# Later normalisations in layer 0, and the sums at the boundary of two layers split anew between VectorE and GpSimd

## The chip, the cores and the metric

The kernel runs on one core of a Trainium2 chip. A core has five engines, each with its own in-order program: TensorE (PE in the profile, its weight loads PEld), VectorE (DVE), ScalarE (ACT), GpSimd (POOL), and SyncE (SP), which here issues nearly all DMAs. Engines wait for each other by semaphores. The metric is the device time of one execution in microseconds.

## The reference

The input `x` is 128 graphs of 64 nodes with 768 features, in float32, and `adj` a 64x64 mask for each graph. Two layers follow each other; both end in a residual and a layer normalisation.

```python
# layer 0, per graph (12 heads of 64)
h    = einsum('bnd,ade->bane', x, W);  th = tanh(h)
attn = th @ w_src + swapaxes(th @ w_dst)          # one score per pair of nodes
attn = where(~adj, -999, leaky(attn, 0.2));  attn = softmax(attn)
out  = elu(attn @ h + b)
gate = sigmoid(x @ H_w.T + H_b)
x    = layernorm(x + gate * out + (1 - gate) * x)
# layer 1, per graph (6 heads of 128)
q, k, v = x @ Wq + bq, x @ Wk + bk, x @ Wv + bv
probs   = softmax(q @ k.T / sqrt(128) + where(adj, 0, -9e15))
x       = layernorm(x + (probs @ v) @ Wf + bf)
```

## The kernel before

**Order.** All work is issued by hand-written step tables: `at(step, f)` puts a function into the list of a step, and `run` (L263) calls the lists in order. Within a step the order of the `at` calls counts. Since every engine is in order, this list is each engine's program; a function put a step later stands behind all that the earlier step issues on the same engine. A step of layer 0 holds one block product of TensorE (six matmul records of 128x384, about 1.94 us); a step of layer 1 has two pairs of 128x256 matmuls.

**Layer 0 (`phase_a`, L308).** The 8192 rows are 64 tiles of 128 rows (two graphs each), taken as 32 pairs. Each pair has three big products: h (with W), the gate, and, once the pair's layer 0 output is there, V (v of layer 1, with Wv). Each is done as a Winograd-form product in 7 block products (`Product`, L197): `matmuls(i)` and `evict(i)`, where ScalarE keeps one operand as `snap` (L418), and VectorE adds (L441 for h and gate, L460 for V). Pairs 0 to 2 start 14 steps apart (there is no V yet), later ones 21.

A tile then runs through the class `Tile0` (L469): tanh (L478), products with w_dst and w_src on GpSimd (L482, L490), the destination scores go through DRAM and come back spread over the rows (L500, L508, `dst_in`), neighbours' values of h come by DMA (`hx`, L518 and L519), twelve additions on ScalarE (L532, in two halves of six), mask and maximum (L539, L543, VectorE), exp (L548, ScalarE), scale by the reciprocal `rs` (L556, L558, GpSimd), probs (transposes on TensorE, L569, copied by L574), aggregate (L587, TensorE), elu (L601 to L615), two mixes with the gate (L620 to L630), the statistics of the norm (`norm1`: L284 to L295 on VectorE, L296 to L301 on GpSimd, which ends in `shift`), the normalisation itself (`norm2`: L305 on ScalarE, L639 on VectorE for the last pair), and the spill of the result to DRAM (`spill`, L647, x_d<-xb). About a pair later `x1_in` reads the rows back (L390, four DMAs of xp<-x_d a tile), they are transposed (L397; L412 and L413 for the last pair), stored as xT_d (L736) and feed the V product, whose results are stored by L461 (v_d<-v). `load(p)` (L337) reads x of a later pair.

**The boundary.** Layer 1's q, k and final products use another bilinear form: a weight has 15 slots of which 14 are sums (`weight15_sum`, L165 to L167; 128x512 elements each, columns of two halves, j = 0 and 1), and the activations have 11 sums (`group_sum`, L844 to L846, for a group of four tiles; `pair_sum`, L858, for pairs ahead of the final product). Before, the 14 sums of Wq run on VectorE and those of Wk on GpSimd, from step o+44 of the last pair (o is its first step), during its V product; the sums of Wf run on GpSimd in layer 1, from step 16. Chunks of the weights come by DMA (`load15`, L156).

**Layer 1 (`phase_b`, L789).** 16 groups, each with 90 steps: q and k of head halves j = 0, then j = 1 (`R` = 15 steps each), then the final products of its predecessor's context. A step's matmuls (L876) read a sum or part; results are taken by ScalarE (`first`, L897) or added by VectorE (`add`, L902). Scores are L941. `load_adj` also makes `fill` (L811) from the mask. For group 0 the sums were spread over its first steps, four steps ahead of the step that needs them; group 1 has six of its sums on VectorE and five on GpSimd, all later groups all on GpSimd. The result buffers `X` in PSUM are shared by both layers and are given out in turn.

Since the change adds lines, some lines stand further down in the changed kernel: L736 becomes L741, L811 L819, L846 L854, L876 L884, L897 L905, L902 L910, L1113 L1125.

Of the kernel before, what the change touches and what calls it, by code (L numbers as in the profile page):

```python
# [12 lines left out]
ALU = mybir.AluOpType  # L13
AX = mybir.AxisListType

P = 128
# [3 lines left out]
L1_NEG = -9000000000000000.0  # L20
# [33 lines left out]
SIGN = {"+": ALU.add, "-": ALU.subtract}  # L54
# [7 lines left out]
def kernel(  # L62
# [84 lines left out]
    def weight15(i):  # L147
        return wts.tile([P, 7, CH, HALF], F32, name=f"w{i}", tag=f"w{i}").rearrange(
            "p s c o -> p (s c o)"
        )[:, : 15 * 2 * 256].rearrange("p (s c o) -> p s c o", s=15, c=2)  # L150

    def load15(wb, src, k):

        kb, c = divmod(k, 2)
        rows = src[k * P : (k + 1) * P, :] if src is Wf else in_order(src)[k]
        nc.sync.dma_start(  # L156
            wb[:, 3 * kb : 3 * kb + 3, c, :], rows.rearrange("p (n o) -> p n o", n=3)
        )
# [3 lines left out]
        r = src.rearrange("(h p c) o -> h c p o", h=2, c=CH)  # L162
        return [r[k // CH, k % CH] for k in range(NC)]

    def weight15_sum(wb, k, eng):  # L165
        to, a, b, sign = WEIGHT_SUMS[k]
        eng.tensor_tensor(wb[:, to], wb[:, a], wb[:, b], SIGN[sign])  # L167

    def weight_sums(part, eng, ks=range(4)):

# [137 lines left out]
    def phase_a(ctx):  # L308
# [24 lines left out]
        def load(p):  # L333
            st[p]["x"] = []
            for i in range(2):
                t = xb[:, (0, 1, 5, 6)[(2 * p + i) % 4]]
                nc.sync.dma_start(t, x_t[2 * p + i])  # L337
                st[p]["x"].append(t)
# [312 lines left out]
        def at(step, *fs):  # L651
            events.setdefault(max(step, 0), []).extend(fs)

        def dense(d, key, i):
            d[key].matmuls(i)
            d[key].evict(i)
# [19 lines left out]
        for p in range(NP):  # L676
            d, o = st[p], O[p]
            d["p"] = p
            if p:
                at(max(o - 20, 1), lambda p=p: load_adj(p))  # L680
                at(o + 8, lambda p=p: load(p))

            def xb_in(d, i):
                d.setdefault("xp", []).append(blocks(x_t[2 * d["p"] + i]))

            def xT(d, i):
                d.setdefault("T", []).append(turn(d["xp"][i]))

            if p:
                at(max(o - 20, 1), lambda d=d: xb_in(d, 0))  # L690
                at(max(o - 16, 1), lambda d=d: xb_in(d, 1))
                at(o - 6, lambda d=d: xT(d, 0))
                at(o - 5, lambda d=d: xT(d, 1))
                at(o - 4, lambda d=d: sums(d))
            else:
                at(0, lambda d=d: d.update(T=[transposed(t) for t in d["x"]]))
                at(0, lambda d=d: sums(d))
            at(o, lambda d=d: start_h(d))
            at(o + 7, lambda d=d: start_g(d))
            for i in range(7):  # L700
                at(o + i, lambda d=d, i=i: dense(d, "W", i))
                at(o + 7 + i, lambda d=d, i=i: dense(d, "G", i))
            for i, s in ((1, o), (0, o + (4 if p == NP - 1 else 5))):
                t = Tile0(p, i)
                at(s + 6 + (i == 0), t.tanh, t.cap)
                at(s + 7, t.dst_mul)
                at(s + 8, t.src_mul)
                at(s + 9, t.dst_sum, t.dst_out)
                at(s + 10, t.src_sum)
                at(s + 13, t.dst_in)  # L710
                at(s + 16, t.exchange)

                at(s + (15 if i else 17), lambda t=t: t.add(0))
                at(s + (16 if i else 17), lambda t=t: t.add(1))
                at(o + (14 if i else 16), t.gate_in)
                at(o + (17 if i else 18), t.gate)
                n = s - (i == 1)
                at(n + 18, t.mask, t.top)
                at(n + 19, lambda t=t: t.exp(0))
                at(n + 20, lambda t=t: t.exp(1))  # L720
                at(s + 21, lambda t=t: t.scale(0), lambda t=t: t.scale(1))
                at(s + 24, t.probs)
                at(s + 25, t.aggregate)
                at(s + 26, t.elu)
                at(s + 27, t.mix1)
                at(s + 28, t.mix2)
                at(s + 29, t.norm1)
                at(s + 30, t.norm2)
                at(s + 31, t.spill)

            def x1_in(d, i):
                d["xp", i] = blocks(x1_d[2 * d["p"] + i])

            def x1T(d, i, t):
                d["x1T", i] = t
                nc.sync.dma_start(xT_d[d["p"]][:, i], t)  # L736

            def x1_sums(d):
                d["T"] = [d["x1T", i] for i in range(2)]
                sums(d)  # L740

            if p < NP - 3:
                v = O[p + 3] + 14
                times = ((1, v - 19, v - 13), (0, v - 16, v - 10))
            elif p < NP - 1:

                v = O[-1] + (21 if p == NP - 3 else 28)
                times = ((1, v - 16, v - 7), (0, v - 15, v - 6)) if p == NP - 3 else (
                    (1, v - 12, v - 7), (0, v - 10, v - 6)
                )  # L750
            if p < NP - 1:
                for i, t0, t1 in times:
                    at(t0, lambda d=d, i=i: x1_in(d, i))
                    at(t1, lambda d=d, i=i: x1T(d, i, turn(d["xp", i])))
                at(times[1][2] + 1, lambda d=d: x1_sums(d))
            else:
                v = o + 45
                for i in range(2):
                    at(o + 43 - i, lambda d=d, i=i: x1T(d, i, transposed(d["x"][i])))
                at(o + 44, lambda d=d: x1_sums(d))  # L760
            at(v, lambda d=d: start_v(d))
            for i in range(7):
                at(v + i, lambda d=d, i=i: dense(d, "V", i))
# [6 lines left out]
        early = []  # L770

        def load_early(i, src, k):
            if k == 0:
                early.append(weight15(i))
            load15(early[i], src, k)

        for k in range(NC):
            at(o + (7 + k if k < 4 else 8 + 2 * k), lambda k=k: load_early(0, Wq, k))
            at(o + 20 + 2 * k, lambda k=k: load_early(1, Wk, k))
        for k in range(len(WEIGHT_SUMS)):  # L780

            at(o + 44 + k // 2, lambda k=k: weight15_sum(early[0], k, nc.vector))
            at(o + 45 + k // 2, lambda k=k: weight15_sum(early[1], k, nc.gpsimd))
        at(o + 30, lambda: load_T4(0))
        run(events, O[-1] + 80)
        return early
# [2 lines left out]
    def phase_b(ctx, wq, wk):  # L789
# [15 lines left out]
        def load_adj(g):  # L805
            d = st[g]
            a = small.tile([P, 2, 2, S], U8, name="adj1")
            for q in range(2):
                nc.sync.dma_start(a[:, q], adj_p[2 * g + q])
            d["fill"] = small.tile([P, 2, 2, S], F32, name="fill1")  # L810
            nc.vector.tensor_scalar(  # L811
                d["fill"], a, 1.0, -L1_NEG, op0=ALU.subtract, op1=ALU.mult
            )

        def load_v(g, q, i):
# [252 lines left out]
        def at(step, *fs):  # L1068
            events.setdefault(max(step, 0), []).extend(fs)
# [4 lines left out]

        R = len(STEPS)
        N = 6 * R
        wf = weight15(2)
        for k in range(NC):
            at(2 + k, lambda k=k: load15(wf, Wf, k))
        for k in range(len(WEIGHT_SUMS)):  # L1080
            at(16 + 2 * k, lambda k=k: weight15_sum(wf, k, nc.gpsimd))
        for g in range(NG):
            d, o = st[g], N * g
            d["S"] = {}
# [1 line left out]
            if g:  # L1086
                at(o - 29 if g > 1 else 14, lambda g=g: load_T4(g))
                at(o - 35, lambda g=g: load_adj(g))
            ready = {}
            for k in range(len(SUMS)):  # L1090


                eng = nc.vector if g == 1 and k in (2, 3, 5, 6, 8, 10) else nc.gpsimd
                if g == 0:

                    t = max(min(SUM_STEPS[k], *(
                        [SUM_STEPS[m] - 1 for m in range(len(SUMS)) if 6 + k in SUMS[m][:2]] or [99]
                    )) - 4, -1)
                    if t < 0:
                        group_sum(d, k, nc.vector)  # L1100
                    else:
                        at(t, lambda d=d, k=k: group_sum(d, k, nc.vector))
                    continue
                if g == 1:

                    t = max([R * 3 + SUM_STEPS[k] + 1] + [ready[r] for r in SUMS[k][:2] if r in ready])
                    ready[6 + k] = t
                else:
                    t = o - 24 + 2 * k
                at(t, lambda d=d, k=k, eng=eng: group_sum(d, k, eng))  # L1110
# [114 lines left out]
```

## Time and profile before

| | us |
|---|---|
| three runs | 2883.85, 2884.47, 2884.81 |
| median | 2884.47 |
| profiled execution, its own time | 2882.71 |
| its span, first to last instruction | 2880.6 |
| TensorE busy in the span | 2825.0 (98%) |
| VectorE / ScalarE / GpSimd busy | 1877.8 / 1201.5 / 1535.4 |
| mean granted TensorE clock | 0.997 |

Layer 0 takes the time up to about 1453 us of the span; its last V product, the weights' sums and the first group's sums lie from there to about 1507. A line of the groups or of a timeline names the engine, the line of the kernel, the operation and its tiles (out<-in); in a timeline the first number is the start, the second the time to the end of the row's last instruction, and square brackets hold the idle time of that engine just before and what ended it. A line of the waits names who waited, for whom, the sum in us, how many times, and the longest.

### The profile page before, as it was taken

To read this page: it belongs to the slowest core of one execution; us is meant where nothing else is said; L and a number is where in the kernel's file an instruction comes from. 1 tells how busy PE (TensorE), PEld (TensorE's weight loads), DVE (VectorE), ACT (ScalarE), POOL (GpSimd) and SP (SyncE) were. 2 spreads that over 40 slices of the span, in tenths; PEclk is the share of its full clock that TensorE was granted. 3 is DMA by queue.
4 is the path that set the end of the run, shared out by engine and by line. 5 is a ranking of instruction groups with operands and counts; after the bars stand their busy time and mean duration, and the time that the engine had idled before them with its cause. 6 is when DMAs were issued, how large, how long until landed. Compare 5 with 4: busy or idle time off the path is not lost.

```text
span 2880.6 us, 50750 instructions
## 1 busy us (share of the span) xinstructions
PE 2825.0 (98%) x18108; PEld 2061.9 (72%) x18108; DVE 1877.8 (65%) x3716; ACT 1201.5 (42%) x3737; POOL 1535.4 (53%) x1633
## 2 busy tenths in 40 slices
PE   8899999999999999999989999999999999999998
PEld 4556566666665665666558888888888888888887
DVE  4787777777877777778675555555555555555556
ACT  4656656566566565565522221222211222211223
POOL 4755655655555565555462555346454456454455
PEclk9999999999999999999999999999999999999999
DMA  6335445344454454443640211212211212211222
GB/s 179 108 107 155 126 134 150 116 146 137 124 146 137 124 155 122 139 143 121 201 147 18 89 69 59 84 56 89 89 65 58 89 56 89 89 61 62 89 83 72
DMA packets 358683, 308.40 MB, mean 107 GB/s; under 512 B 226592, under 2 KB 304160, under 8 KB 358432
## 3 DMA queue, kind: packets, MB, share of 16 engines
q1 hardware_dynamic: 358432, 305.16, 34.5%
q8 instruction: 144, 2.36, 0.3%
q14 instruction: 107, 0.88, 0.1%
HBM read 191.41 MB, written 101.06 MB: 102 GB/s over the span
## 4 chain that ended last, share of the span: by engine, by line
PE 86%; DVE 6%; POOL 3%; DMA 2%; issue 1%; ACT 1%; SPq 1%; DVEq 0%; POOLq 0%; ACTq 0%
PE X L876 42%; PE X L209 37%; PE pb L1016 2%; PE pb L941 2%; PE pa L587 2%; PE pa L569 1%; DVE z L629 1%; PE pb L996 1%; DVE z L620 1%; DVE S L846 0%; DVE w L173 0%; POOL th L490 0%; POOL w L173 0%; DVE st L284 0%; DVE xb L630 0%
## 5 line engine op out<-in xcount | busy, mean ns | idle before, releaser
L209 PE MATMUL X<-w,S 128*128 128x384 f32 x2304 | 800.8, 493 | 18.2 <-ACT snap L418 7.4
L876 PE MATMUL X<-S,w 128*128 128x256 f32 x2816 | 667.0, 383 | 7.2 <-DVE S L846 5.9
L209 PEld LDWEIGHTS X<-w,S 128*128 128x128 f32 x2304 | 430.6, 191 | 309.4 <-ACT snap L418 18.4
L209 PE MATMUL X<-w,T 128*128 128x384 f32 x1728 | 596.1, 487 | 6.0 <-ACT snap L418 3.5
L876 PEld LDWEIGHTS X<-S,w 128*128 128x128 f32 x2816 | 525.5, 190 | 82.2 <-DVE S L846 7.3
L209 PEld LDWEIGHTS X<-w,T 128*128 128x128 f32 x1728 | 326.1, 191 | 229.4 <-ACT snap L418 7.8
L858 POOL TENSOR_TENSOR Sc<-cT 128x256 f32<-128x256 f32 x224 | 161.7, 729 | 405.4 <-PE X L876 392.0
L876 PE MATMUL X<-w,Sc 128*128 128x256 f32 x1408 | 322.5, 381 | 0.9 <-DVE xs L919 0.8
L919 DVE TENSOR_TENSOR xs<-xs,X 128x256 f32<-128x256 f32 x512 | 210.6, 420 | 169.0 <-PE X L876 160.3
L876 PEld LDWEIGHTS X<-w,Sc 128*128 128x128 f32 x1408 | 265.4, 190 | 38.7 <-DVE xs L919 1.6
L548 ACT ACTIVATE s<-s,nmx 128x64 f32<-128x64 f32 x768 | 256.2, 335 | 76.8 <-DVE nmx L543 76.8
L902 DVE TENSOR_TENSOR k<-k,X 128x256 f32<-128x256 f32 x320 | 133.7, 421 | 216.0 <-PE X L876 166.1
L902 DVE TENSOR_TENSOR q<-q,X 128x256 f32<-128x256 f32 x320 | 133.2, 420 | 179.7 <-PE X L876 146.0
L305 ACT ACTIVATE xs<-xs,shift,rstd 128x768 f32<-128x768 f32 x62 | 63.5, 1025 | 419.0 <-POOL shift L301 412.4
L876 PE MATMUL X<-xb,w 128*128 128x256 f32 x960 | 236.6, 379 | 0.0
L897 ACT ACTIVATE k<-X,bk_c 128x256 f32<-128x256 f32 x192 | 91.1, 474 | 306.9 <-PE X L876 306.8
L897 ACT ACTIVATE q<-X,bq_c 128x256 f32<-128x256 f32 x192 | 91.1, 474 | 284.3 <-PE X L876 284.3
L482 POOL TENSOR_TENSOR tmp<-th,wd_bc 128x768 f32<-128x768 f32 x64 | 141.4, 2210 | 126.8 <-ACT th L478 126.8
L296 POOL TENSOR_TENSOR rstd<-rstd,neg_half 128x1 f32<-128x1 f32 x126 | 69.3, 550 | 247.4 <-DVE rstd L295 246.3
L532 ACT ACTIVATE s<-s,src 128x64 f32<-128x64 f32 x768 | 193.3, 335 | 15.0 <-DMA s<-dst_d 14.4
L876 PEld LDWEIGHTS X<-xb,w 128*128 128x128 f32 x960 | 181.2, 190 | 24.0
L418 ACT COPY snap<-X 128x384 f32<-128x384 f32 x288 | 134.8, 468 | 101.3 <-PE X L209 99.5
(119 smaller groups left out, 4110.3 us busy)
## 6 DMA issues: line engine op xcount, KB each, us to landing
xb<-in_x_dram SPq DMA_DIRECT2D x64, 384.0 KB
s<-dst_d SPq DMA_DIRECT2D x128, 192.0 KB
x_d<-xb SPq DMA_DIRECT2D x64, 384.0 KB
xT_d<-T SPq DMA_DIRECT2D x64, 384.0 KB
v_d<-v SPq DMA_DIRECT2D x128, 192.0 KB
xb<-xT_d SPq DMA_DIRECT2D x32, 768.0 KB
xb<-v_d SPq DMA_DIRECT2D x256, 96.0 KB
xs<-x_d SPq DMA_DIRECT2D x64, 384.0 KB
```

Source lines behind the costliest of these rows:

```text
L209: nc.tensor.matmul(o, self.lhsT(i, c), rhs, start=first and c == 0, stop=last and c == CH - 1, skip_group_check=True,)
L296: nc.gpsimd.tensor_tensor(rstd, rstd, neg_half, ALU.pow)
L305: nc.scalar.activation(r, r, AF.Identity, bias=shift, scale=rstd)
L418: nc.scalar.copy(t, ps)
L482: nc.gpsimd.tensor_tensor(self.tmp, self.th, wd_bc, ALU.mult)
L532: nc.scalar.activation(self.s[:, a], self.s[:, a], AF.Prelu, bias=self.src[:, a : a + 1], alpha=LEAKY_ALPHA,)
L548: nc.scalar.activation(self.s[:, a], self.s[:, a], AF.Exp, bias=self.nmx[:, a : a + 1], accum_out=self.sm[:, a : a + 1],)
L858: nc.gpsimd.tensor_tensor(t, pair_part(d, q, r0), pair_part(d, q, r1), op)
L876: nc.tensor.matmul(ps, self.lhsT(r, slot, c), self.rhs(r, slot, c), start=start and c == 0, stop=stop and c == 1, skip_group_check=True,)
L897: nc.scalar.activation(o[:, b], ps, AF.Identity, bias=bias[:, hd : hd + 1], scale=1.0 if positive else -1.0)
L902: nc.vector.tensor_tensor(o[:, b], o[:, b], ps, ALU.add if positive else ALU.subtract)
L919: nc.vector.tensor_tensor(o, o, ps, ALU.add if positive else ALU.subtract)
```

## The change

In layer 0 `norm2` and `spill` move a step later for all pairs but the last; the scale of tile 1 goes to the front of its step; x of the next pair is loaded two steps later; the x1 loads of pair 30 come one or two steps earlier and its transposes one later. Wk's chunks are loaded in a rotated order, the first chunk last, at step o+48. At the boundary VectorE sums only the first 128 columns (j = 0) of Wq's slots; the second half of Wq and both of Wk are summed by GpSimd at the start of layer 1, as 42 sums of 128x256; Wf's sums move from step 16 to step 40. Group 0's 11 sums are all issued on VectorE ahead of the first step of q, in the order in which they are needed; `fill` becomes a function of its own, at step 26 of each group.

```diff
         r = src.rearrange("(h p c) o -> h c p o", h=2, c=CH)
         return [r[k // CH, k % CH] for k in range(NC)]
-    def weight15_sum(wb, k, eng):
+    def weight15_sum(wb, k, eng, o=slice(0, 256)):
         to, a, b, sign = WEIGHT_SUMS[k]
-        eng.tensor_tensor(wb[:, to], wb[:, a], wb[:, b], SIGN[sign])
+        eng.tensor_tensor(wb[:, to, :, o], wb[:, a, :, o], wb[:, b, :, o], SIGN[sign])
     def weight_sums(part, eng, ks=range(4)):
...
         def at(step, *fs):
             events.setdefault(max(step, 0), []).extend(fs)
+        def at_front(step, *fs):
+            events.setdefault(step, [])[:0] = fs
+
         def dense(d, key, i):
             d[key].matmuls(i)
             d[key].evict(i)
...
             d["p"] = p
             if p:
                 at(max(o - 20, 1), lambda p=p: load_adj(p))
-                at(o + 8, lambda p=p: load(p))
+                at(o + 10, lambda p=p: load(p))
             def xb_in(d, i):
                 d.setdefault("xp", []).append(blocks(x_t[2 * d["p"] + i]))
...
                 at(n + 18, t.mask, t.top)
                 at(n + 19, lambda t=t: t.exp(0))
                 at(n + 20, lambda t=t: t.exp(1))
-                at(s + 21, lambda t=t: t.scale(0), lambda t=t: t.scale(1))
+                (at_front if i else at)(s + 21, lambda t=t: t.scale(0), lambda t=t: t.scale(1))
                 at(s + 24, t.probs)
                 at(s + 25, t.aggregate)
                 at(s + 26, t.elu)
                 at(s + 27, t.mix1)
                 at(s + 28, t.mix2)
                 at(s + 29, t.norm1)
-                at(s + 30, t.norm2)
-                at(s + 31, t.spill)
+
+                n = s + (0 if p == NP - 1 else 1)
+                at(n + 30, t.norm2)
+                at(n + 31, t.spill)
             def x1_in(d, i):
                 d["xp", i] = blocks(x1_d[2 * d["p"] + i])
...
                 v = O[-1] + (21 if p == NP - 3 else 28)
                 times = ((1, v - 16, v - 7), (0, v - 15, v - 6)) if p == NP - 3 else (
-                    (1, v - 12, v - 7), (0, v - 10, v - 6)
+                    (1, v - 13, v - 6), (0, v - 12, v - 5)
                 )
             if p < NP - 1:
                 for i, t0, t1 in times:
...
         early = []
         def load_early(i, src, k):
-            if k == 0:
+            if len(early) == i:
                 early.append(weight15(i))
             load15(early[i], src, k)
         for k in range(NC):
             at(o + (7 + k if k < 4 else 8 + 2 * k), lambda k=k: load_early(0, Wq, k))
-            at(o + 20 + 2 * k, lambda k=k: load_early(1, Wk, k))
+
+            at(o + (48 if k == 5 else 20 + 2 * k), lambda k=k: load_early(1, Wk, (k + 1) % NC))
         for k in range(len(WEIGHT_SUMS)):
-            at(o + 44 + k // 2, lambda k=k: weight15_sum(early[0], k, nc.vector))
-            at(o + 45 + k // 2, lambda k=k: weight15_sum(early[1], k, nc.gpsimd))
+            at(o + 44 + k // 2, lambda k=k: weight15_sum(early[0], k, nc.vector, slice(0, P)))
         at(o + 30, lambda: load_T4(0))
         run(events, O[-1] + 80)
         return early
...
             a = small.tile([P, 2, 2, S], U8, name="adj1")
             for q in range(2):
                 nc.sync.dma_start(a[:, q], adj_p[2 * g + q])
+            d["adj"] = a
+
+        def fill(d):
             d["fill"] = small.tile([P, 2, 2, S], F32, name="fill1")
             nc.vector.tensor_scalar(
-                d["fill"], a, 1.0, -L1_NEG, op0=ALU.subtract, op1=ALU.mult
+                d["fill"], d["adj"], 1.0, -L1_NEG, op0=ALU.subtract, op1=ALU.mult
             )
         def load_v(g, q, i):
...
         R = len(STEPS)
         N = 6 * R
+
+        def need(k):
+
+            return min([SUM_STEPS[k]] + [
+                need(m) - 0.5 for m in range(len(SUMS)) if 6 + k in SUMS[m][:2]
+            ])
+
         wf = weight15(2)
         for k in range(NC):
             at(2 + k, lambda k=k: load15(wf, Wf, k))
+        for wb, j in ((wk, 0), (wq, 1), (wk, 1)):
+            for k in range(len(WEIGHT_SUMS)):
+                weight15_sum(wb, k, nc.gpsimd, slice(j * P, (j + 1) * P))
         for k in range(len(WEIGHT_SUMS)):
-            at(16 + 2 * k, lambda k=k: weight15_sum(wf, k, nc.gpsimd))
+            at(40 + 2 * k, lambda k=k: weight15_sum(wf, k, nc.gpsimd))
         for g in range(NG):
             d, o = st[g], N * g
             d["S"] = {}
...
             if g:
                 at(o - 29 if g > 1 else 14, lambda g=g: load_T4(g))
                 at(o - 35, lambda g=g: load_adj(g))
+            at(o + 26, lambda d=d: fill(d))
             ready = {}
-            for k in range(len(SUMS)):
+            for k in sorted(range(len(SUMS)), key=need) if g == 0 else range(len(SUMS)):
                 eng = nc.vector if g == 1 and k in (2, 3, 5, 6, 8, 10) else nc.gpsimd
                 if g == 0:
-
-                    t = max(min(SUM_STEPS[k], *(
-                        [SUM_STEPS[m] - 1 for m in range(len(SUMS)) if 6 + k in SUMS[m][:2]] or [99]
-                    )) - 4, -1)
-                    if t < 0:
-                        group_sum(d, k, nc.vector)
-                    else:
-                        at(t, lambda d=d, k=k: group_sum(d, k, nc.vector))
+                    group_sum(d, k, nc.vector)
                     continue
                 if g == 1:
```

## The prediction

> **What bounds the kernel now.** The page's first part and windows by stage (columns: stretch, its length, busy us and instructions of each engine, TensorE clock, DMA share, GB/s):
>
> ```profile
> PE 2825.0 (98%) x18108; PEld 2061.9 (72%) x18108; DVE 1877.8 (65%) x3716; ACT 1201.5 (42%) x3737; POOL 1535.4 (53%) x1633
> ...
> 60.00:200.00 140.00, 123.63 (x750) 72.14 (x749) 108.68 (x162) 93.85 (x348) 91.56 (x82) 0.96 0.38 111
> 200.00:1400.00 1200.00, 1199.80 (x6360) 722.12 (x6351) 912.62 (x1419) 747.10 (x2597) 685.77 (x654) 1.00 0.46 136
> 1400.00:1453.20 53.20, 46.99 (x248) 28.07 (x246) 36.63 (x59) 26.52 (x98) 20.64 (x21) 1.00 0.71 221
> 1453.20:1507.40 54.20, 44.40 (x163) 31.71 (x164) 40.39 (x46) 10.03 (x21) 45.68 (x31) 0.94 0.43 136
> 1521.90:1539.10 17.20, 15.26 (x111) 12.85 (x109) 9.88 (x22) 2.84 (x6) 6.30 (x5) 1.00 0.01 1
> 1539.10:2780.00 1240.90, 1240.84 (x9454) 1074.56 (x9453) 677.52 (x1789) 271.10 (x522) 610.93 (x747) 1.00 0.22 74
> ```
>
> TensorE is busy for all of 200 to 1400 and 1539 to 2780: there the change can move nothing. It can act in four gaps: 16.4 us idle in the opening, 6.2 ahead of the last values, 9.8 around the phase boundary, 1.9 in the second k product. The waits of TensorE in the opening and the boundary name the owners:
>
> ```profile
> PE X L209 <- ACT snap L418: 10.3, 5, 3.6
> PE X L209 <- POOL s L558: 3.3, 1, 3.3
> ...
> PE X L876 <- DVE S L846: 5.9, 4, 4.1
> PE X L209 <- DVE v L460: 2.6, 1, 2.6
> PE X L876 <- DVE k L902: 1.1, 1, 1.1
> ```
>
> The timelines of ScalarE in the opening, then of all engines at the boundary, show how:
>
> ```profile
> 126.94 1.03 ACT L305 ACTIVATE xb<-xb,shift,rstd 128x768 f32<-128x768 f32 x1 [5.66 <-POOL shift L301]
> 127.88 1.53 ACT L532 ACTIVATE s<-s,src 128x64 f32<-128x64 f32 x6
> 129.31 0.46 ACT L418 COPY snap<-X 128x384 f32<-128x384 f32 x1
> ...
> 1456.90 23.02 POOL L167 TENSOR_TENSOR w<-w 128x512 f32<-128x512 f32 x14
> 1457.93 9.16 DVE L167 TENSOR_TENSOR w<-w 128x512 f32<-128x512 f32 x6
> 1467.70 3.74 PE L209 MATMUL X<-w,S 128*128 128x384 f32 x6 [2.60 <-DVE v L460]
> 1473.70 5.09 DVE L846 TENSOR_TENSOR S<-xb 128x512 f32<-128x512 f32 x3
> 1475.50 3.40 PE L876 MATMUL X<-S,w 128*128 128x256 f32 x8 [4.06 <-DVE S L846]
> ```
>
> The snap that TensorE needs stands behind a normalisation held 5.66 us by GpSimd. At the boundary each VectorE sum takes about 1.6 us, as long as GpSimd's beside it, though the line's last sums, alone, take 0.68.
>
> **What the Trainium skill says.** "SBUF — State Buffer", section "SBUF: two separate sides": VectorE with two SBUF operands and GpSimd share an exclusive lock, held for a whole instruction. The trace agrees in kind: 9.16/6 = 1.53 us against 0.68 alone; not in size, since 0.68 + 1.27 (GpSimd's 128x512 alone) would be 1.95 and pairs show 1.67. "TensorE: Matmul & The Clock Gate", section "What's actually happening": an idle window slows the clock until TensorE has been busy a while. Six matmuls after the 2.60 us wait took 3.74 us, and 2.10 without one. "DMA: Bandwidth & Descriptors", section "Anatomy of one DMA": a DMA's wait sits on the issuing sequencer, and a transfer has a fixed cost of about 2 us; SP's rows agree (a spill landed 2.53 us after issue).
>
> **The change, part by part** (minus is faster).
>
> *Normalisation a step later, opening.* It removes no instruction; L305 now stands behind its step's snap. The five snap waits come to 2.64, 3.63, 0.55, 3.12 and 3.28 = 13.2 us, and two of them cost 1.6 us each in slow clock: 16.4 at most. What is late next is not TensorE's own: pairs start every 14 steps here, VectorE is busy 108.7 of 140 us, and the normalisation's output still feeds transposes, sums and the next pair through GpSimd (L558 and L301) and SP. Following these chains wait by wait, with durations from the same rows, I get TensorE 2.5 us earlier after the first wait, still 2.6 after the third, and 4.5 by 190 us. Behind 200 us TensorE is gapless, so the gain is kept: −4.5; bounds 0 and −16.4.
>
> *x1 loads and spill, pairs 30 and 31.* The spill of tile 60 now comes after tile 61's four L390 loads on SP; tile 60's own four loads must wait for it to land (2.53 us), and behind these on SP stand hx (L518, L519), a Wq chunk and the last pair's L508 (s<-dst_d). So L508 is later by one L390 group, 2.64 us, and some 2 of the landing: 4.7. ScalarE's L532 already waits for that DMA (1.99 us at 1420.08); after it come mask, L548, probs and the aggregate at 1428.8, each waiting for the one before. Less 0.3 for a mask (L539) that meets less GpSimd work: +4.4; bounds 0 (other slack takes it) and +6.
>
> *Last values to the second q.* From the start of the last V product (1453.22):
> - Before, V ends after 18.2 us (1471.44). After, VectorE's half-width sums have no GpSimd sums beside them: some 0.4 us each in place of 1.53 to 1.67, so the add L460 is no longer late and the 2.60 wait with its 1.9 of slow clock goes: 7 x 1.94 plus entry, 13.85. −4.4.
> - The first group sum still waits for V's last matmul, because it takes the buffer that V frees. So no sum runs during the values; TensorE idles as before.
> - Now all 11 sums precede the first q add, and TensorE's step 5 waits for an add behind them. GpSimd meanwhile does 42 half-sums, 128x256, 0.73 us alone (L858). The lock's overlap per pair was 1.95 − 1.67 = 0.28; the same share of 0.73 + 0.68 = 1.41 gives a pair in about 1.13 us. First sum at 13.85 + 1.35 = 15.2, ten more 11.3, an add 0.42: step 5 at 27.0. Before: 1482.78, 29.56.
> - Then ten q steps at 0.865 = 8.65 and 1.7 of slow clock after the long wait, k in 13.0 (14.27 before, 1.1 of it the wait on L902, caused by the fill that now comes later): second q at 50.4 against 54.1. −3.7 in all. Bounds from the pace of a sum, ten of them: at 0.68 each 4.5 us less and no slow clock, −9.9; at 1.67 each 5.4 more and 1.0 more of slow clock, +2.7.
>
> GpSimd's deadlines hold: 42 half-sums from about 1462 end by 1498 at 0.85 each, Wk's first 14 by 1476 (needed at 1490), Wq's second by 1488 (1503). If they slipped, TensorE would wait one for one.
>
> *The second k.* Wf's 14 sums, from step 40 by twos, share GpSimd with group 1's sums and keep it busy for 20 us, where it had 6.3 busy of 17.2. VectorE's six group-1 sums here then take 1.67 in place of 0.68: 6 x 0.99 = 5.9, less the 1.2 of the fill that left and less the slack of adds: the last k add ahead of the scores is 10.05 us after step 9, before 6.6. +3.4; bounds 0 and +4.5. Wf is needed only at step 150.
>
> *At nothing:* fill in later groups, the scale put first, x loads (two steps later; the residual that reads them is 19 steps on): TensorE's gapless stretches cover them; uncovered, a scale would cost its 0.83 us. Wk's last chunk is issued behind the last V's first store; GpSimd's first half-sum waits for it, inside the margin above.
>
> Sum: −4.5 + 4.4 − 3.7 + 3.4 = −0.4, on a profiled run of 2882.71 (span 2880.6). The median is 1.8 above that run; −0.3 on it: **2884.2 us**.
>
> **Rivals.**
> - *The opening obeys TensorE's waits alone.* The whole 16.4 returns instead of 4.5: 2884.2 − 11.9 = 2872.3. For: snap is the largest wait. Against: VectorE would be busy 108.7 of 123.6 us, and L558 and L569 waits of 3.3 and 1.8 stand beside it.
> - *VectorE isn't held by GpSimd's short sums.* 0.68 a sum at the start is 4.5 less; at the second k, with half of its pairs, some 2 less: 2877.7. For: the unpaired sums. Against: every pair in the boundary's rows is stretched.
> - *Slower: the hold doesn't shrink with GpSimd's instruction.* The sums keep 1.67: ten times 0.54 is +5.4, and the slow clock after a longer idle +1: 2890.6. It ends slower than before from 1.17 a sum on (0.4/10 above 1.13), and beyond 0.2% (5.8 us, about what a measurement can tell from no change) from some 1.65. For: the 1.6 us rows. Against: 128x256 alone is 0.73.
> - *It doesn't do what it says:* group sums during the last values cannot start; already in the numbers.
>
> **How the numbers follow.** Four terms that cancel: 0.50, own range 2878.7 to 2890. First rival 0.17, second 0.15, third 0.18. Faster by over 0.2%: the first rival and the second (6.5 us), 0.32; slower 0.18; between 0.50. Range 2871 to 2892: it takes in the middle of each rival and leaves out a good third of the outer two and the tails of the likeliest, some 0.18.
>
> **What would show it.** Right: no PE wait on snap L418 over 2 us in 60 to 200, but waits on others there; the last pair's first L508 about 4.7 us later, counted from its products' start, and the aggregate with it; V's last product without the 2.6 wait; group sums of about 1.1 us in a row of 11; TensorE waiting some 9 us in all for them; scores of the first group waiting on L910's k add. Wrong: an opening that gains over 8 us, or sums at 0.7 or 1.6.

## The result, and the profile after

The changed kernel takes 2888.75 us (median of 20 runs), the kernel before 2884.14 in the same comparison: a ratio of 1.0015, 95% interval 1.0008 to 1.0022. It is slower by some 4.6 us; the forecast was 2884.2, no change that could be measured. The profiled execution has a span of 2885.7 us, 5.1 more than before.

The page's first part:

```profile
PE 2829.1 (98%) x18108; PEld 2063.7 (72%) x18108; DVE 1864.8 (65%) x3716; ACT 1199.1 (42%) x3737; POOL 1551.0 (54%) x1661
```

The windows by stage (columns as before):

```profile
60.00:200.00 140.00, 126.13 (x767) 74.11 (x766) 114.28 (x173) 97.50 (x351) 96.19 (x87) 0.99 0.39 107
200.00:1400.00 1200.00, 1197.65 (x6335) 719.00 (x6334) 906.81 (x1408) 741.88 (x2593) 688.10 (x650) 1.00 0.47 136
...
1521.90:1543.00 21.10, 17.69 (x110) 14.44 (x109) 13.13 (x22) 2.84 (x6) 19.85 (x14) 0.84 0.01 2
```

The opening does hold more work (767 matmuls in 140 us, before 750). But from 200 to 1400 us, where TensorE had done 6360 matmuls, it now does 6335. GpSimd is busy for 19.85 of the 21.1 us of the second k, before for 6.30 of 17.2.

Every kernel here issues the same 18108 matmuls in the same order, so TensorE's n-th matmul can be set beside the n-th of the first profile of before. This table is worked out from that: how much each stage became longer (+) or shorter (−), in us, with a second profile of the kernel before (the last run below) as a measure of chance.

| stage, us of the profile before | forecast | changed | before again |
|---|---|---|---|
| up to 18 | 0 | −0.4 | −1.6 |
| opening, 18 to 191 | −4.5 | −5.6 | −1.6 |
| layer 0, 191 to 1418 | 0 | **+4.8** | −0.4 |
| last pair, 1418 to 1439 | +4.4 | +4.0 | +1.9 |
| last values to second q, 1439 to 1516 | −3.7 | −2.9 | +0.8 |
| second k, 1516 to 1539 | +3.4 | +4.1 | 0.0 |
| rest | 0 | +0.8 | +1.4 |

One row stands out: the long stage that the forecast took for gapless. TensorE's waits in the changed kernel, in 60 to 200, in 200 to 1400, and in 1440 to 1560 us:

```profile
PE X L209 <- ACT snap L418: 4.4, 4, 2.0
PE X L209 <- DVE hp L441: 2.9, 1, 2.9
PE pa L569 <- POOL s L558: 2.8, 5, 1.0
...
PE X L209 <- ACT snap L418: 1.9, 6, 0.6
PE pa L587 <- ACT pt L574: 0.4, 1, 0.4
...
PE X L884 <- DVE q L910: 5.9, 1, 5.9
PE X L884 <- DVE k L910: 3.2, 2, 2.1
PE X L884 <- DVE S L854: 1.5, 2, 1.1
```

Before, the same question for 200 to 1400 gives no wait at all; now TensorE waits for snap in several pairs. Each is small, and more is lost than the rows hold, because the first matmul after such a wait is 0.43 us from the next instead of 0.32, and the shortest waits aren't listed. From 191 us on TensorE's lead goes from 6.0 to 1.2 us, by 0.1 to 0.9 at a time, mostly at one place in the pair, though not in every pair (1.4 us go in one, at 276 to 279). SP's timeline of one pair, before and then changed, shows what comes late:

```profile
1141.50 0.38 SPq L647 DMA_DIRECT2D x_d<-xb  x1
1143.52 2.57 SPq L390 DMA_DIRECT2D xp<-x_d  x4
...
1148.62 1.12 SPq L508 DMA_DIRECT2D s<-dst_d  x2
```

```profile
1141.37 2.57 SPq L390 DMA_DIRECT2D xp<-x_d  x4
1144.04 0.55 SPq L647 DMA_DIRECT2D x_d<-xb  x1
...
1146.91 1.13 SPq L508 DMA_DIRECT2D s<-dst_d  x2
```

TensorE runs 2.15 us earlier here. L390 is 2.15 earlier too, but L508 only 1.71: the spill, a step later, stands between. ScalarE of the same pair, before and then changed, with TensorE's wait at the end:

```profile
1152.69 2.98 ACT L532 ACTIVATE s<-s,src 128x64 f32<-128x64 f32 x12 [0.37 <-DMA s<-dst_d]
...
1159.74 0.46 ACT L418 COPY snap<-X 128x384 f32<-128x384 f32 x1
```

```profile
1151.46 2.97 ACT L532 ACTIVATE s<-s,src 128x64 f32<-128x64 f32 x12 [1.31 <-DMA s<-dst_d]
...
1158.52 0.45 ACT L418 COPY snap<-X 128x384 f32<-128x384 f32 x1
1159.02 1.24 PE L209 MATMUL X<-w,T 128*128 128x384 f32 x3 [0.19 <-ACT snap L418]
```

Behind L532 on ScalarE come a snap, the exps and the next snap. Before, that snap ended at 1160.20 and its matmul began at 1160.82: it had 0.62 us to spare, which is its slack. Now TensorE waits for it. From L508 to L532 were 4.07 us and are 4.55 in this pair, but that is not the rule: over the 26 pairs of the long stage's middle the mean is 4.33 before and 4.44 now, while L508 is issued 0.50 us later against TensorE. So the order on SP makes most of the delay, and a slower transfer behind the spill some 0.1. ScalarE's waits in 200 to 1400 us sum this up, before and then changed:

```profile
ACT s L532 <- DMA s<-dst_d: 9.9, 19, 1.2
```

```profile
ACT s L532 <- DMA s<-dst_d: 29.3, 27, 2.3
```

That the spill's place on SP does this is the theory; the rival is that the later x loads (L337), or `norm2` itself, cost the time.

### The profile page after: what moved, and what is told of

Its sections match the earlier page's. It is cut to its first block, busy times and chain, and to the rows that moved or that the text cites. A ratio compares the mean times of both kernels' runs of the same rounds, so it can differ in the third digit from the quotient of the medians.

```text
span 2885.7 us, 50796 instructions
## 1 busy us (share of the span) xinstructions
PE 2829.1 (98%) x18108; PEld 2063.7 (72%) x18108; DVE 1864.8 (65%) x3716; ACT 1199.1 (42%) x3737; POOL 1551.0 (54%) x1661
## 4 chain that ended last, share of the span: by engine, by line
PE 83%; DVE 7%; POOL 3%; DMA 2%; ACT 2%; issue 1%; SPq 1%; DVEq 0%; POOLq 0%; ACTq 0%
PE X L884 42%; PE X L209 34%; PE pb L1024 2%; PE pb L949 2%; PE pa L587 1%; PE pa L569 1%; DMA s<-dst_d 1%; ACT s L532 1%; DVE z L629 1%; PE pb L1004 1%; ACT s L548 1%; DVE S L854 1%; DVE z L620 1%; DVE st L284 1%; DVE s L539 1%
## 5 line engine op out<-in xcount | busy, mean ns | idle before, releaser
L532 ACT ACTIVATE s<-s,src 128x64 f32<-128x64 f32 x768 | 193.1, 335 | 38.7 <-DMA s<-dst_d 38.7
```

The source lines that it names most:

```text
L532: nc.scalar.activation(self.s[:, a], self.s[:, a], AF.Prelu, bias=self.src[:, a : a + 1], alpha=LEAKY_ALPHA,)
```

## The experiments

The kernel before takes 2883.7 to 2884.2 us beside these runs. A stage's figure is, as in the table, against the first profile of before.

**The spill a step earlier.**

```diff
-                at(n + 31, t.spill)
+                at(s + 31, t.spill)
```

> The changed kernel with the spill (L647) issued one step earlier again, right behind the later norm2, so that SP has it ahead of the x1 loads (L390) as before; all else as changed. Theory (the spill behind the four x1 loads makes the second tile's s<-dst_d late in every pair, and L532, the exps and the snap behind them): TensorE's waits for snap between 200 and 1400 us go from 1.9 us to nothing, ScalarE's wait for s<-dst_d there falls from 29 us towards the 10 of the kernel before, the 4.7 us that the opening's gain loses by 1337 us stay, and pair 30's loss of 4.1 goes too: about 2880 us, 4 below the kernel before. Rival (the x loads two steps later, or norm2 itself, cause it): the loss between 200 and 1400 stays, and only pair 30's 4.1 goes: about 2884.6.

2883.21 us, ratio 0.9998 (0.9990 to 1.0006), 5.5 below the changed kernel. The stage from 191 to 1418 costs +0.1 in place of +4.8, no PE wait is listed from 200 to 1400, and ScalarE's wait is that of before:

```profile
ACT s L532 <- DMA s<-dst_d: 10.1, 20, 1.2
```

So the theory holds for the long stage. The last pair keeps 2.5 us that I expected to go.

**x loaded at o+8 again.** `load(p)` puts pair p's rows for the residual where pair p−2 has its result. In this kernel it does so ahead of the later spill of tile 0 in the first two pairs, so that other data are stored there; the amount of work is the same.

> The changed kernel with x loaded at o+8 as before in place of o+10. Theory (the spill's place is the cause): nothing moves, about 2888.7 us, the loss between 200 and 1400 us is still 4 to 5. Rival (the two L337 transfers ahead of the spill and of s<-dst_d are the cause): that loss goes, about 2884.

2891.13 us, ratio 1.0024 (1.0015 to 1.0032); the long stage costs +4.9. The rival falls. That the kernel is 2.4 us slower than the changed one, where I expected no difference, stays unexplained.

**The spill earlier for pair 30 alone** (`at(s + 31 if p == NP - 2 else n + 31, t.spill)`).

> The changed kernel with the spill of pair 30 alone a step earlier again, ahead of its x1 loads. Theory (the step on pairs 30 and 31 in the prediction): the last pair's second s<-dst_d is about 4.7 us earlier, TensorE's 4.7 us wait for snap at 1422 and the late aggregate go, 4.1 us less: about 2884.6; the loss between 200 and 1400 us stays. Rival (the x1 reads moved to earlier steps set it, not the spill): within 1 us of the changed kernel, 2888.

2887.69 us, 1.0013 (1.0006 to 1.0021). The long stage still costs +4.2. The last pair costs 2.3 in place of 4.0, where I expected nothing: a miss, and the time is about where the rival put it. SP has the spill first, but then all eight L390 of both tiles in a row (5.46 us) ahead of L508, and L532 begins 5.6 us after that (1417.89 to 1423.53). The x1 loads' own steps matter too.

**Wf's sums at step 64.**

```diff
-            at(40 + 2 * k, lambda k=k: weight15_sum(wf, k, nc.gpsimd))
+            at(64 + 2 * k, lambda k=k: weight15_sum(wf, k, nc.gpsimd))
```

> The changed kernel with Wf's 14 sums from step 64 by twos in place of step 40, after the second k. Theory (GpSimd's Wf sums beside VectorE's six group-1 sums stretch these from 0.68 to about 1.4 us and make the last k adds and the scores late): the sums fall to 0.7 us, TensorE's waits for k (3.2 us in all) go, 3.9 us less: about 2884.9. Rival (group 1's own five GpSimd sums are what holds VectorE, or the fill moved): the waits stay, 2888.

2886.84 us, 1.0010 (1.0004 to 1.0017): half of what I expected. The second k costs +1.9 in place of +4.1. The timeline shows why:

```profile
1534.01 0.68 DVE L854 TENSOR_TENSOR S<-xb 128x512 f32<-128x512 f32 x1
...
1536.67 10.55 POOL L167 TENSOR_TENSOR w<-w 128x512 f32<-128x512 f32 x7
1537.29 1.63 DVE L854 TENSOR_TENSOR S<-xb,S 128x512 f32<-128x512 f32 x1
```

A step number holds nothing back on an engine that waits for nothing: once GpSimd's own sums are done, it starts on Wf at once, still beside VectorE's last sums.

**Wf's sums at step 16, as before.**

> The changed kernel with Wf's 14 sums back at steps 16 to 42. Theory (they meet group 1's sums only because they are issued past step 40; issued earlier, GpSimd runs them right behind its half-sums, while VectorE has only adds from PSUM): GpSimd has finished them by about 1520 us, VectorE's group-1 sums take 0.68 us, the second k loses nothing against the kernel before, 3.9 us less than changed: about 2884.9. Rival (the fill or the half-sums are what makes the second k late): it still loses 3 or more, 2888.

2884.66 us, 1.0001 (0.9993 to 1.0009), 4.1 below the changed kernel. The second k costs −0.2: this term is shown. GpSimd has Wf done before group 1's sums.

**Spill and pair 30's x1 loads as before** (the first run's edit, and `(1, v - 12, v - 7), (0, v - 10, v - 6)`).

> The changed kernel with the spill a step earlier, as in the first run of this study, and with pair 30's x1 loads and transposes at their old steps as well. Theory (what is left of the last pair's lateness, 2.5 us there, is the second tile's four x1 loads now ahead of the last s<-dst_d on SP and in the queues): s<-dst_d lands as in the kernel before, the 3.2 us wait for snap at 1419 and the slow clock after it go, TensorE keeps 4.6 us against the kernel before up to the last V product: about 2880.7, 2.4 below the first run. Rival (the later norm2 alone makes it late): as in the first run, 2883.

2882.01 us, 0.9989 (0.9983 to 0.9996), 1.2 below the first run, which is half of what I expected and within the noise of the two. In the profile the 3.2 us wait for snap is gone, as expected. The last pair still costs 2.1, from another cause: matmuls at half clock behind the wait on L587. The last run shows that this comes and goes in the kernel before.

**These three put back together.**

> The edits of the first, fifth and sixth run together: the later normalisations and the new boundary, but the spill, pair 30's x1 loads and Wf's sums where they were. If the stages add up as the theory has them: 4.6 from the opening and 2.8 from the boundary, nothing lost in between: about 2876.5, 0.9974 of the kernel before. If the parts only trade waits, no lower than the best of its parts, about 2881.

2877.96 us, 0.9977 (0.9968 to 0.9987). The parts add up: −5.7 opening, −0.1 long stage, −2.9 boundary, −0.2 second k; the last pair's 2.3 of slow clock is what the forecast of 2876.5 had not.

**Wk in whole sums on GpSimd.**

```diff
-        for wb, j in ((wk, 0), (wq, 1), (wk, 1)):
+        for wb, o in ((wk, slice(0, 2 * P)), (wq, slice(P, 2 * P))):
             for k in range(len(WEIGHT_SUMS)):
-                weight15_sum(wb, k, nc.gpsimd, slice(j * P, (j + 1) * P))
+                weight15_sum(wb, k, nc.gpsimd, o)
```

> The changed kernel with Wk summed by GpSimd in 14 instructions of 128x512 in place of 28 of 128x256, ahead of Wq's 14 halves. Theory (a pair of sums on VectorE and GpSimd takes some 0.8 of both alone): VectorE's 11 sums, beside 1.27 us instructions, take 1.6 to 1.67 us in place of 1.13, TensorE's step 5 is 5 us later, and the time about 2893. Rival (the pace is VectorE's own, or the lock's per instruction whatever its length): 1.13 us stays and the time is 2888 to 2889.

2898.54 us, 1.0043 (1.0030 to 1.0057). A sum on VectorE, and TensorE's step 5 behind the last of them, first in the timeline of the changed kernel, then here:

```profile
1479.87 1.21 DVE L854 TENSOR_TENSOR S<-xb 128x512 f32<-128x512 f32 x1
...
1482.59 2.08 PE L884 MATMUL X<-S,w 128*128 128x256 f32 x4 [5.92 <-DVE q L910]
```

```profile
1487.00 1.75 DVE L854 TENSOR_TENSOR S<-S,xb 128x512 f32<-128x512 f32 x1
...
1491.39 2.08 PE L884 MATMUL X<-S,w 128*128 128x256 f32 x4 [7.52 <-DVE q L910]
```

A sum starts every 1.13 us beside GpSimd's 128x256, every 1.67 beside its 128x512; in this run too the last two sums step at 1.13, when GpSimd has gone on to its halves. The pace follows the length of GpSimd's instruction. The time is 5.5 us above what I expected: step 5 comes 7.0 us later, counted from V's last product, and not 5, since VectorE's last Wq sums are stretched as well (some 1.25 us in place of 0.7), and the rest isn't accounted for.

**`norm2` alone on the kernel before**, with x loaded at o+10 and the spill at its step.

> The kernel before with norm2 a step later and x loaded two steps later, and nothing else: the spill stays at its step, behind norm2; loads of x1, sums and weights as before. Theory (the opening's gain is that of the snap no longer queued behind a normalisation, and it is kept if s<-dst_d isn't delayed): TensorE 4.5 to 6.8 us earlier by 190 us and through to 1417, the boundary as before: 2878 to 2879.5. Rival (the gain comes from the scale put first in its step, or the gain erodes whatever SP does): 2882 or more.

2878.94 us, 0.9979 (0.9971 to 0.9987). TensorE is 7.0 us ahead at 191 us (1.5 of it from the load of the first weights) and 7.4 at 1418. The part that the change is named for does gain, if the spill stays, and it needs neither the scale put first nor the new boundary.

**The boundary alone**, layer 0 in its old order.

> The changed kernel with layer 0's order as before (norm2, spill, scale, x and x1 loads), the boundary and Wf's sums as changed. If the stages are independent: no loss up to the last V product, 2.8 less up to the second k, 3.9 more in it: 1.1 above the kernel before, about 2885.2. If the later x1 loads of layer 0 are what the boundary needs, it loses more, 2888.

2886.46 us, 1.0006 (0.9998 to 1.0015): the boundary −2.1, the second k +4.2, as for independent stages; the sum can't be told from no change.

**Group 0's sums spread again**, on top of the three edits put back.

```diff
-                    group_sum(d, k, nc.vector)
+                    t = int(need(k)) - 4
+                    if t < 0:
+                        group_sum(d, k, nc.vector)
+                    else:
+                        at(t, lambda d=d, k=k: group_sum(d, k, nc.vector))
```

> The run that put the spill, pair 30's x1 loads and Wf's sums where they were, with group 0's 11 sums again spread, four steps ahead of the step that needs each, the half-sums kept. Theory (with a sum every 1.13 us VectorE's chain of sums sets the pace either way, but all sums ahead of the first add leave ten steps of q for after the chain, 5.9 us of idle TensorE and its slow clock): steps run between the sums, the second q starts 3 to 4 us earlier, about 2874.5. Rival (the adds put between the sums delay the last ones as much as the steps gain): 2877 to 2879.

2869.34 us, 0.9945 (0.9933 to 0.9958): 8.6 below the run without it, about twice what I expected, and the best kernel here. The boundary costs −9.9 in place of −2.9. TensorE's waits there:

```profile
PE X L884 <- DVE q L910: 1.4, 1, 1.4
```

The wait of 5.9 is 1.4. Two sums of this run, the first behind another sum, the second behind an add:

```profile
1473.11 1.21 DVE L854 TENSOR_TENSOR S<-xb 128x512 f32<-128x512 f32 x1
...
1474.58 0.88 DVE L854 TENSOR_TENSOR S<-xb,S 128x512 f32<-128x512 f32 x1
```

A sum that follows an add on VectorE takes 0.81 to 0.88 us, and 1.10 to 1.21 behind another sum (presumably because GpSimd's instruction passes during the add, which reads PSUM; that was only argued). This makes the adds between the sums cheap, but it does not shorten the chain: from the start of V's last product to the end of the last sum it takes 16.0 us with four adds in it, and took 14.7 without. The 7.0 us that the boundary gains are on TensorE: 4.5 of the wait, and 2.5 because the ten steps of q behind it take 8.7 us and not 11.2, with no half clock. The expectation let the chain of sums set the pace to the end; behind step 5 TensorE doesn't wait for it at all. Of the 9.2 us between these two profiles the boundary has 7.0 and the last pair's slow clock, absent here, 2.3.

**The kernel before again**, one execution.

> The kernel before once more, for a second profile: what differs between two executions of one kernel can't be credited to an edit. If the 2 us that runs with layer 0's old order lose at the last pair (six matmuls at half clock behind the wait on L587) come by chance, this profile may show them or not, and all else agrees with the first within 0.5 us a stage, the opening included. If the first profile of before is as all are, they are absent, and the edits cause them.

2883.2 us. TensorE in the first profile of before, behind L587, then in this one:

```profile
1428.81 0.27 PE L587 MATMUL pa<-hp,pt 64*64 64x64 f32 x1 [3.13 <-DMA v_d<-v]
1429.76 2.20 PE L209 MATMUL X<-w,T 128*128 128x384 f32 x6
```

```profile
1425.46 0.27 PE L587 MATMUL pa<-hp,pt 64*64 64x64 f32 x1 [3.19 <-ACT pt L574]
1426.42 3.89 PE L209 MATMUL X<-w,T 128*128 128x384 f32 x6
```

The same work after nearly the same wait takes 2.20 or 3.89 us. So of the last pair's +4.0, up to 2 can be chance, and so can 1.6 of the opening, where the clock fell at other places (I had expected 0.5 at most). The second profile has neither the long stage's loss nor the second k's.

What looks like chance can be read from the clock records of the traces. Within an execution the granted clock changes only at multiples of 3.41 us from one another. In the second profile one such stretch, 1423.1 to 1426.5, holds most of the wait: TensorE is idle for 68% of it, and the next stretch is granted half clock. In the first profile the wait is split over two stretches, idle for 44% and 47%, and the clock stays full. In the 14 profiles there are 170 stretches of full clock between 60 and 1600 us in which TensorE is idle for a quarter or more. All 70 that are idle for 58% or more are followed by half clock, and none of the 95 below 55%; the five between go both ways. So it matters how a wait lies against these stretches, and that differs between two executions of one kernel.

## Why the prediction was wrong

Taking the mean over all profiles of kernels that share an order, against those with the old one: opening −4.9 against −1.0, so −3.9; long stage +4.1 against −0.1; last pair +5.0 (five profiles with both the later spill and the earlier x1 loads) against +1.5, so +3.5; last values to second q −2.3 against +0.6, so −2.9; second k +4.1 against 0. The sum is about +5, and the medians differ by 4.6.

- **Opening, −4.5: right.** The snap waits went from 10.3 to 4.4 us, and others took their place (hp L441 from 0.5 to 2.9, v L460 from 0.4 to 2.5). The rival that all 16.4 return is excluded. One reading in it is wrong: its five snap waits of 13.2 us count in the 3.28 for L558; the five come to 10.3, as its own row says. The −4.5 doesn't rest on this sum.
- **"Behind 200 us TensorE is gapless, so the gain is kept": the step that failed.** It judged by idle time and not by slack. A gapless TensorE says that nothing comes too late now, not how far things are from coming too late. The slack can be read in the trace of before: at the eight places of the long stage where TensorE waits for snap in the changed kernel (the row above has the six longest), that snap had ended 0.05 to 0.91 us ahead of its matmul. And the prediction priced what the spill is moved past on SP for pairs 30 and 31 alone, though `n = s + 1` moves it in every pair but the last. What the runs show in its place is +4.2 from 191 to 1418 us, 0.15 us a pair on the mean of 28 pairs, as much as the opening gives; with the spill alone put back it is +0.1.
- **Pairs 30 and 31, +4.4: near in size** (+3.5), with L508 4.6 us later against TensorE (4.7 told). But TensorE stops ahead of the aggregate, for the snap behind L532 (4.7 us), which the prediction's chain left out here too. And there are two causes, of which I named the spill as the main one: it is 2 us or so, the x1 loads' earlier steps about 1 more, and the half clock after the waits is not steady enough to say more.
- **Last values to the second q, −3.7: right in mechanism, 0.8 too good.** V's wait of 2.6 is gone, the sums step at 1.13 us as estimated, step 5 comes 26.6 us after V's start (27.0 told). The 0.8 is slow clock: the ten steps of q behind the long wait take 11.65 us, 3.0 more than at full clock, where 1.7 was told. The 1.13 was reached by taking off the same 0.28 us, and not, as the text says, the same share, which gives 1.21; the runs bear out the first. Both rivals on the pace, 0.68 and 1.67, are excluded for half-sums. What the prediction did not ask is whether the sums should stand ahead of the adds: issuing all 11 first costs some 7 us against spreading them.
- **Second k, +3.4: right in cause, in size with help.** +4.1, and gone when Wf is back at step 16. The six sums take 1.1 to 1.6 us and not 1.67; TensorE's waits grow by 1.5 us, and some 2.2 are half clock behind them, which the sum had not.
- **The chances:** the likeliest case's own range reached to 2890 and so held 2888.75, but that is luck: it was built round terms that cancel. They don't: with +4.2 in place of nothing it would have been 2888.4, slower by less than 0.2%, which is what was measured.

## What to carry to other kernels

When a step is moved, list what it passes on every queue in each iteration that moves, steady state included, and ask for the slack there, the time between the end of what is waited for and the need of it. An engine without gaps has no visible wait, but may have, as here, less than a microsecond of slack. A step number doesn't delay work on an engine that isn't waiting for anything; if work is to miss a stage, put it ahead of that stage or behind a real dependency. Where VectorE's and GpSimd's sums held each other up, shorter instructions on GpSimd made VectorE's faster (one every 1.13 us in place of 1.67), and TensorE's steps did better between the sums than after the last of them (−9.9 us in place of −2.9).

## What was not expected of the hardware

With VectorE's 128x512 sums (0.68 us alone) beside GpSimd's, a sum starts every 1.13 us where GpSimd's instruction takes 0.73 and every 1.67 where it takes 1.27: in both cases GpSimd's time and 0.40, so about 0.28 of VectorE's sum overlaps. "SBUF — State Buffer" of the Trainium skill, section "SBUF: two separate sides", has the one that comes second fully blocked until the other's instruction ends; the difference between the cases agrees with a lock held for GpSimd's whole instruction, the 0.28 does not, and where it comes from is open. And TensorE's clock was halved after waits shorter than a stretch of 3.41 us: idle for 58% of one was enough in every case here, so that waits of 3.13 and 3.19 us, in two executions of one kernel, had different ends.
